# Feed-forward of an attention layer: the second product in row tiles of 128 tokens with a column-tiled remainder

## The chip, the cores and the metric

The program runs on one core of a Trainium2 chip. A core has five engines that run their own instruction streams: TensorE (PE; its weight loads are listed apart as PEld), VectorE (DVE), ScalarE (ACT), GpSimd (POOL) and SyncE (SP), which only issues transfers here. Work passes through an on-chip memory of 128 partitions (SBUF), and TensorE writes its results into a second one (PSUM) of eight banks of 128 partitions by 512 fp32 numbers. Sixteen DMA engines move data between these and the chip's main memory, or within SBUF. Engines wait for one another, and for transfers, on semaphores.

The metric is the time of the whole program on the device in microseconds (us). Before the change three runs gave a median of 3563.27 us, from 3559.06 to 3570.37.

## The reference

Four layers run one after another on x, 16 batches of 100 tokens of 512 channels, all in fp32. Layers 0 and 2 are cross-attentions to a context of 361 tokens a batch, layers 1 and 3 are recurrent layers (a scan over the 100 tokens, with decays, and a channel mixing). The change lies in the last part of layer 2, its feed-forward:

```python
hidden = out + residual
residual = hidden
y = layer_norm(hidden, ln2_w, ln2_b)
y = jax.nn.gelu(y @ fc_w + fc_b, approximate=True)   # 512 -> 2048
y = y @ proj_w + proj_b                              # 2048 -> 512
return residual + y
```

The inputs are a full draw: every weight, bias and scale has values of its own, so nothing of this can be left out.

## The kernel before, in words

The residual x stays in SBUF through all layers as 16 tiles `xb[b]` of 100 partitions (the tokens of a batch) by 512 channels. `layer2_ffn` works on four groups of four batches (`NG = 4`, `G = 4`), so on T = 400 tokens at a time. For each group it does the following.

1. `ln_to_channels` normalizes the four tiles on VectorE (lines 206, 207 and 219) and GpSimd (lines 208 and 209), turns them on TensorE (line 226) so that channels lie on partitions, and evicts the four results to `yT` on ScalarE with scale and bias (line 229).
2. The first product: for each of 16 blocks f of 128 hidden channels, `project` (line 63) adds up four matmuls with 128 columns of `fc` as weights and the 400 tokens as the moving data. ScalarE takes each result through the gelu into `h[:, f, :]` (line 1607). `h` has hidden channels on partitions and the 400 tokens as columns, and one buffer.
3. The second product: for each batch i of the group, `project` adds up 16 matmuls over f. Here the weights are the 100 columns of `h` that belong to the batch, and the moving data are the 512 columns of `proj[:, f, :]`; the result in PSUM has the tokens of the batch on 100 partitions, as `xb` has. GpSimd adds the bias row to x (line 1612), and VectorE adds the result from PSUM to x (line 1617).

Every PSUM result of this stage takes one of eight banks in turn (`mm_tile`). A matmul of fp32 operands in the code is two instructions on TensorE, each with a weight load.

The order of instructions on each engine within this stage is not that of the code: a scheduler places them by their dependences and priorities, so that statistics and normalized rows of later groups are computed on VectorE while the first group is still under way. On TensorE the order is the plain one: transposes, first product, second product of group 0, then of group 1, and so on.

SyncE's queue holds, in this order around the stage: the four loads of `proj` (line 1585) and the small ones, layer 3's Wk, then Wv, Wr, Wg and Wo (line 57), each of which waits for a buffer that a quarter of `fc` holds until the last group's first product has read it, and then what layer 3 begins with: `vec` (line 633), two parts of `maa_w` (lines 655 and 657), `td_w2` and a part of `maa_w2` (lines 660 and 661), `td_w1` (663), `st01` (665) and the state `s0` (667). These take the SBUF space of layer 2's feed-forward, so the first of them waits for the last matmul of the stage.

Layer 3 (`rwkv`) begins with constants on VectorE (lines 680 to 709), the statistics of the first four batches on VectorE and GpSimd (line 77 with the tiles `st_a`, `mv_a`, `ve_a`, `rstd_a`), a rearrangement of `s0` on TensorE (line 82, tile mm) that ScalarE copies to `s0r`, and then, next in ScalarE's queue, the normalized rows `xn_a`.

In the profile's lines a tile is written without its numbers: `p` is the result of the second product, `h` both the first product's bank and the tile it is evicted to, `l_fc` and `l_proj` the weights, `av` the weighted sum of values in layer 2's attention (`attend`), which is computed by groups of 32 columns of weights that go to four different groups of 32 PSUM partitions.

Of the kernel before, what the change touches and what calls it, by code (L numbers as in the profile page):

```python
# [9 lines left out]
F32 = mybir.dt.float32  # L10
U8 = mybir.dt.uint8
AF = mybir.ActivationFunctionType
ALU = mybir.AluOpType
AX = mybir.AxisListType

B, L, E, S2 = 16, 100, 512, 361
NC = E // 128
G = 4
NG = B // G
T = G * L  # L20
# [15 lines left out]
def xattn_sequence(ctx: ExitStack, tc: tile.TileContext, d: dict, out: bass.AP):  # L36
    nc = tc.nc
# [6 lines left out]
    def psum_bank(es, name, bufs):  # L44
        pool = es.enter_context(tc.tile_pool(name=name, bufs=bufs, space=PSUM))
        return lambda n: pool.tile([128, 512], F32, tag="mm", name=n)
# [13 lines left out]
    def project(ps, lhs, rhs, n=NC):  # L60

        for c in range(n):
            nc.tensor.matmul(out=ps, lhsT=lhs(c), rhs=rhs(c), start=(c == 0), stop=(c == n - 1))  # L63
# [148 lines left out]
    def ln_to_channels(pool, g, w, bb, dst, eps, name, bank):  # L212

        rows = [xb[g * G + i] for i in range(G)]
        mv, rstd = ln_stats(pool, rows, eps, name)
        xn = []
        for i in range(G):
            t = pool.tile([L, E], F32, tag="xn", bufs=G + 1, name=f"xn_{name}_{i}")
            nc.vector.tensor_scalar(
                t, rows[i], mv[:, i, 0:1], rstd[:, i : i + 1], ALU.subtract, ALU.mult  # L220
            )
            xn.append(t)
        for c in range(NC):
            ps = bank(f"lnT_{name}_{c}")
            for i in range(G):
                nc.tensor.transpose(
                    ps[:, i * L : (i + 1) * L], xn[i][:, c * 128 : (c + 1) * 128], ident[:L, :L]
                )
            nc.scalar.activation(  # L229
                dst(c), ps[:, :T].rearrange("p (b t) -> p b t", t=L), AF.Identity,  # L230
                bias=bb[:, c : c + 1], scale=w[:, c : c + 1],
            )
# [1056 lines left out]
    def l2_vecs(pool):  # L1289
        t = pool.tile([128, len(L2_VECS), NC], F32, tag="vec2", name="vec2")  # L1290
        nc.sync.dma_start(out=t, in_=d["L2_vec"])
        return {k: t[:, i, :] for i, k in enumerate(L2_VECS)}
# [285 lines left out]
    def layer2_ffn(fc, next_weights):  # L1578
        with ExitStack() as es:
            one = es.enter_context(tc.tile_pool(name="l2b_one", bufs=1))  # L1580
            two = es.enter_context(tc.tile_pool(name="l2b_two", bufs=2))
            mm_tile = psum_bank(es, "l2b_mm", 8)
            proj = one.tile([128, 16, E], F32, name="l2_proj")
            for i in range(4):
                nc.sync.dma_start(
                    out=proj[:, 4 * i : 4 * i + 4, :],
                    in_=d["L2_proj_w"][i * 512 : (i + 1) * 512, :].rearrange("(c p) n -> p c n", p=128),
                )
            vec = l2_vecs(one)
            fcb = one.tile([128, 16], F32, name="fcb")  # L1590
            nc.sync.dma_start(out=fcb, in_=d["L2_fc_b"])
            row = one.tile([L, E], F32, name="l2_pb")
            nc.sync.dma_start(out=row, in_=d["L2_proj_b"].partition_broadcast(L))
            for g in range(NG):
                yT = two.tile([128, NC, T], F32, tag="yT", name=f"yTb_{g}")
                ln_to_channels(
                    two, g, vec["ln2_w"], vec["ln2_b"],
                    lambda c: yT[:, c, :].rearrange("p (b t) -> p b t", t=L), 1e-5, f"l2b_{g}", mm_tile,
                )
                h = two.tile([128, 16, T], F32, tag="h", bufs=1, name=f"h_{g}")  # L1600
                for f in range(16):
                    ps = mm_tile(f"h_{g}_{f}")
                    o = (f % 4) * 128
                    project(
                        ps[:, :T], lambda c: fc[f // 4][:, c, o : o + 128], lambda c: yT[:, c, :]
                    )
                    nc.scalar.activation(
                        h[:, f, :], ps[:, :T], AF.Gelu_apprx_tanh, bias=fcb[:, f : f + 1], scale=1.0
                    )
                for i in range(G):  # L1610
                    x = xb[g * G + i]
                    nc.gpsimd.tensor_tensor(x, x, row, ALU.add)
                    ps = mm_tile(f"p_{g}_{i}")
                    project(
                        ps[:L, :], lambda f: h[:, f, i * L : (i + 1) * L], lambda f: proj[:, f, :], 16
                    )
                    nc.vector.tensor_tensor(x, ps[:L, :], x, ALU.add)  # L1617
            return next_weights()

    def load(layer, *names):  # L1620
# [7 lines left out]
        load_w(d["L2_fc_w"][:, i * 512 : (i + 1) * 512], f"l2_fc{i}") for i in range(4)  # L1628
    ])
    ws3 = layer2_ffn(fc, lambda: load(3, "Wk", "Wv", "Wr", "Wg", "Wo"))  # L1630
    rwkv(3, ws3, lambda: {"": None}, True)

# [64 lines left out]
```

## Time and profile before

| quantity | value |
|---|---|
| runs, median (lowest to highest) | 3563.27 us (3559.06 to 3570.37) |
| the profiled execution's own time | 3563.91 us |
| its span, first to last instruction | 3561.8 us |
| mean granted TensorE clock | 0.937 |
| TensorE busy | 3252.8 us (91% of the span) |
| VectorE, ScalarE, GpSimd busy | 1768.5, 972.8, 1374.2 us |
| second product of layer 2's feed-forward on TensorE | 220.4 us, 512 instructions |
| first product | 175.4 us, 512 instructions |
| stage, first transposes to last matmul | 2294.4 to 2704.1 us |

Busy times overlap among engines and don't add up to the span. A group of instructions is given with its busy time, the mean duration of one instruction, and the time for which its engine was idle before it, with what ended that. Matmuls overlap in TensorE's pipeline: the duration of one (593 ns for 512 columns) is longer than the distance from one start to the next (429 ns). So durations of single matmuls are not added up; the distance of starts is used.

### The profile page before, as it was taken

To read this page: it belongs to the slowest core of one execution; us is meant where nothing else is said; L and a number is where in the kernel's file an instruction comes from. 1 tells how busy PE (TensorE), PEld (TensorE's weight loads), DVE (VectorE), ACT (ScalarE), POOL (GpSimd) and SP (SyncE) were. 2 spreads that over 40 slices of the span, in tenths; PEclk is the share of its full clock that TensorE was granted. 3 is DMA by queue.
4 is the path that set the end of the run, shared out by engine and by line. 5 is a ranking of instruction groups with operands and counts; after the bars stand their busy time and mean duration, and the time that the engine had idled before them with its cause. 6 is when DMAs were issued, how large, how long until landed. Compare 5 with 4: busy or idle time off the path is not lost. (4 is left out here: it accounts for less than half of the span.)

```text
span 3561.8 us, 45408 instructions
## 1 busy us (share of the span) xinstructions
PE 3252.8 (91%) x17411; PEld 1434.5 (40%) x17411; DVE 1768.5 (50%) x3570; ACT 972.8 (27%) x1699; POOL 1374.2 (39%) x1036
## 2 busy tenths in 40 slices
PE   6999998868999988989999999699998899998898
PEld 3444443334333333334455455344443433333333
DVE  4777777723767755523333333400001386775551
ACT  1323222322333333322222322201111233333332
POOL 1444444543666655412212112200002366665541
PEclk8999999978999989989999999899998899998998
DMA  5010101022434342011000010200011243434300
GB/s 167 21 30 21 30 21 33 1 65 82 134 101 136 116 130 77 14 52 35 19 19 19 27 31 21 74 0 0 0 47 49 83 138 101 136 116 119 86 27 16
DMA packets 151074, 213.26 MB, mean 60 GB/s; under 512 B 22942, under 2 KB 131294, under 8 KB 150858
## 3 DMA queue, kind: packets, MB, share of 16 engines
q1 hardware_dynamic: 127818, 177.59, 17.3%
q10 hardware_dynamic: 23040, 32.78, 2.6%
q8 instruction: 137, 2.24, 0.3%
q14 instruction: 79, 0.65, 0.1%
HBM read 174.25 MB, written 36.04 MB: 59 GB/s over the span
## 5 line engine op out<-in xcount | busy, mean ns | idle before, releaser
L77 POOL TENSOR_TENSOR a<-a,rr 128x800 f32<-128x800 f32 x256 | 480.5, 1878 | 342.1 <-DVE a L77 265.4
L77 DVE TENSOR_TENSOR_SCAN a<-wr,vb 128x400 f32<-128x400 f32 x512 | 475.7, 970 | 19.3 <-PE acc L82 9.7
L77 DVE TENSOR_TENSOR vb<-vb,kr 128x792 f32<-128x792 f32 x256 | 250.5, 979 | 197.1 <-ACT vb L77 195.5
L77 DVE CUSTOM_DVE_ANT_0 junk<-l_sc,mask 100x361 f32<-100x361 f32 x512 | 273.0, 533 | 89.9 <-PE l_sc L82 73.4
L82 PE MATMUL vb<-vc,sel 32*128 32x396 f32 x1024 | 260.8, 566 | 2.4 <-ACT th L77 1.3
L77 DVE TENSOR_TENSOR pt<-l_sc,maskT 121x400 f32<-121x400 f32 x384 | 193.5, 566 | 91.9 <-PE l_sc L82 91.0
L77 ACT ACTIVATE pt<-pt 121x1600 f32<-121x1600 f32 x96 | 147.6, 1538 | 284.2 <-DVE pt L77 282.6
L1425 DVE CUSTOM_DVE_ANT_0 junk<-l2a_sc,mask 100x361 f32<-100x361 f32 x256 | 136.9, 535 | 173.0 <-PE l2a_sc L82 155.8
L63 PE MATMUL p<-l_proj,h 128*100 128x512 f32 x512 | 220.4, 593 | 0.0
L77 POOL TENSOR_TENSOR xj<-tm,ext 128x400 f32<-128x400 f32 x160 | 152.5, 960 | 170.3 <-DVE tm L77 165.2
L77 DVE SCALAR_TENSOR_TENSOR tm<-mm,vec,sx 128x400 f32<-128x400 f32 x160 | 99.8, 631 | 229.3 <-PE mm L82 184.3
L1617 DVE TENSOR_TENSOR x<-p,x 100x512 f32<-100x512 f32 x16 | 11.1, 691 | 379.3 <-PE p L63 340.2
L1461 POOL TENSOR_TENSOR pa<-pt,pt 121x1600 f32<-121x1600 f32 x16 | 57.2, 3573 | 366.7 <-ACT pt L1456 366.7
L63 PE MATMUL h<-yTb,l_fc 128*128 128x400 f32 x512 | 175.4, 505 | 7.9 <-ACT yTb L229 7.9
L82 PE MATMUL v<-l_v_w,ct 128*121 128x512 f32 x384 | 179.9, 614 | 0.0
L82 PE MATMUL k<-ct,l_k_w 128*128 128x361 f32 x512 | 172.8, 481 | 7.7 <-DVE mv_l2a L207 7.7
L77 POOL TENSOR_TENSOR pa<-pt,pt 121x1600 f32<-121x1600 f32 x32 | 114.7, 3583 | 167.0 <-ACT pt L77 167.0
L82 PE MATMUL l_sc<-kz,qz 32*100 32x361 f32 x1024 | 116.0, 523 | 42.6 <-DVE pt L77 21.6
L77 ACT COPY vb<-s0r 128x8 f32<-128x8 f32 x256 | 43.1, 168 | 408.7 <-PE vb L82 318.6
L82 PEld LDWEIGHTS vb<-vc,sel 32*128 32x128 f32 x1024 | 85.3, 190 | 145.5 <-issue 105.3
L63 PEld LDWEIGHTS p<-l_proj,h 128*100 128x100 f32 x512 | 85.7, 167 | 133.2 <-issue 132.6
L63 PEld LDWEIGHTS h<-yTb,l_fc 128*128 128x128 f32 x512 | 98.4, 193 | 82.9 <-ACT yTb L229 9.8
(254 smaller groups left out, 5317.3 us busy)
## 6 DMA issues: line engine op xcount, KB each, us to landing
kr<-dk SPq DMA_DIRECT2D x256, 100.0 KB
wr<-dw SPq DMA_DIRECT2D x256, 100.0 KB
rr<-dr SPq DMA_DIRECT2D x256, 100.0 KB
ct<-in_ctxT SPq DMA_DIRECT2D x32, 722.0 KB
dk<-k ACTq DMA_DIRECT2D x32, 200.0 KB
kc<-dk SPq DMA_DIRECT2D x32, 200.0 KB
dw<-wd ACTq DMA_DIRECT2D x32, 200.0 KB
dv<-v ACTq DMA_DIRECT2D x32, 200.0 KB
```

Of the source, the lines that this page charges most:

```text
L63: nc.tensor.matmul(out=ps, lhsT=lhs(c), rhs=rhs(c), start=(c == 0), stop=(c == n - 1))
L77: return lambda *args, **kw: tc.keep_in_program_order(op(*args, **kw))
L82: pin(nc.tensor.matmul(**kw))
L1425: nc.vector.tensor_tensor_reduce(out=junk, in0=ss[r][:L, :S2], in1=t["mask"], scale=-1.0, scalar=FLT_MAX, op0=ALU.add, op1=ALU.min, accum_ ...
L1461: nc.gpsimd.tensor_tensor(t["pa"], t["pt"][0], pt, ALU.add)
L1617: nc.vector.tensor_tensor(x, ps[:L, :], x, ALU.add)
```

## The change

The second product no longer follows the batches. Its 400 tokens a group are cut into three tiles of 128 rows and a remainder of 16.

- Each of the three tiles is added up over f with 128 columns of `h` as weights. ScalarE copies the result from PSUM to a tile `po` in SBUF (three buffers), and transfers on SyncE's queue bring its rows to where their batches have them, in a tile `pb` of 100 partitions by four batches by 512 (one buffer). Each tile has tokens of two batches, so there are two transfers a tile: 100 and 28 rows, 72 and 56, 44 and 84.
- The remainder takes the last 32 columns of `h` as weights (16 of them are computed a second time and not used). Its 512 output columns are cut into four quarters r, and the matmul of quarter r writes PSUM partitions 32r to 32r + 31: four column groups of the array, each with its own copy of the weights and 128 columns of `proj` as moving data. ScalarE copies the 128x128 result to a tile `pr`, and four transfers of 16 rows by 128 columns bring the quarters to `pb`.
- VectorE's adds read `pb` in SBUF in place of the PSUM bank, after GpSimd's add of the bias row as before.

```diff
+                pb = two.tile([L, G, E], F32, tag="pb", bufs=1, name=f"pb_{g}")
+                for i in range(3):
+                    ps = mm_tile(f"p_{g}_{i}")
+                    project(
+                        ps, lambda f: h[:, f, i * 128 : (i + 1) * 128], lambda f: proj[:, f, :], 16
+                    )
+                    t = two.tile([128, E], F32, tag="po", bufs=3, name=f"po_{g}_{i}")
+                    nc.scalar.copy(t, ps)
+                    for b in range(G):
+                        lo, hi = max(b * L, i * 128), min(b * L + L, i * 128 + 128)
+                        if lo < hi:
+                            nc.sync.dma_start(
+                                out=pb[lo - b * L : hi - b * L, b, :], in_=t[lo - i * 128 : hi - i * 128, :]
+                            )
+                ps = mm_tile(f"p_{g}_3")
+                for f in range(16):
+                    for r in range(4):
+                        nc.tensor.matmul(
+                            out=ps[32 * r : 32 * r + 32, :128], lhsT=h[:, f, T - 32 : T],
+                            rhs=proj[:, f, r * 128 : (r + 1) * 128], start=(f == 0), stop=(f == 15),
+                        )
+                t = two.tile([128, 128], F32, tag="pr", name=f"pr_{g}")
+                nc.scalar.copy(t, ps[:, :128])
+                for r in range(4):
+                    nc.sync.dma_start(
+                        out=pb[L - 16 : L, G - 1, r * 128 : (r + 1) * 128], in_=t[32 * r + 16 : 32 * r + 32, :]
+                    )
                 for i in range(G):
                     x = xb[g * G + i]
                     nc.gpsimd.tensor_tensor(x, x, row, ALU.add)
-                    ps = mm_tile(f"p_{g}_{i}")
-                    project(
-                        ps[:L, :], lambda f: h[:, f, i * L : (i + 1) * L], lambda f: proj[:, f, :], 16
-                    )
-                    nc.vector.tensor_tensor(x, ps[:L, :], x, ALU.add)
+                    nc.vector.tensor_tensor(x, pb[:, i, :], x, ALU.add)
```

The order of instructions moves as follows. On TensorE only the matmuls of the second product change. ScalarE has the four copies of a group between the last gelu of that group and the first eviction of the next group's transposes. SyncE has the ten transfers of each of groups 0 to 2 between the loads of layer 3's Wk and Wv; of group 3 the six transfers of whole tiles stand behind Wo, then comes `vec`, then the four transfers of the remainder, then `maa_w` and the others to `s0`. On VectorE the add of batch 15 moves behind layer 3's constants, and stands just ahead of layer 3's first statistics; the adds of batches 3 and 7 move behind normalized rows of later groups. GpSimd's order is the same.

## The prediction

> **What bounds the kernel now.** I read the groups of instructions first, to see on which engine the changed lines lie, then the timeline of the stage, then the place where it hands over to layer 3. First the groups inside the feed-forward (line, engine, operation; busy us and mean ns; then the idle time before them and what ended it):
>
> ```profile
> L63 PE MATMUL p<-l_proj,h 128*100 128x512 f32 x512 | 220.4, 593 | 0.0
> L63 PE MATMUL h<-yTb,l_fc 128*128 128x400 f32 x512 | 175.4, 505 | 7.9 <-ACT yTb L229 7.9
> L1607 ACT ACTIVATE h<-h,fcb 128x400 f32<-128x400 f32 x64 | 38.0, 593 | 132.2 <-PE h L63 132.2
> L1617 DVE TENSOR_TENSOR x<-p,x 100x512 f32<-100x512 f32 x16 | 11.1, 691 | 379.3 <-PE p L63 340.2 <-PE lnT_l2b L226 39.1
> ```
>
> TensorE is never idle before a matmul of the second product; every other engine waits for it. Each fp32 matmul of the program is two instructions (256 in the code, x512 here). The timeline of TensorE over one group of four batches (start us, duration):
>
> ```profile
> 2450.40 55.10 PE L63 MATMUL p<-l_proj,h 128*100 128x512 f32 x128
> 2505.33 1.54 PE L226 MATMUL lnT_l2b<-ident,xn_l2b 100*128 100x100 f32 x16
> 2506.71 43.18 PE L63 MATMUL h<-yTb,l_fc 128*128 128x400 f32 x128
> 2549.72 55.10 PE L63 MATMUL p<-l_proj,h 128*100 128x512 f32 x128
> ```
>
> There is no gap: second product 54.93 us (2505.33 - 2450.40), transposes 1.38, first product 43.01, and again. The stretch from 2451 to 2506 has a granted clock of 1.00. So this stage is bound by TensorE, and what is taken from it there comes off the end, unless the hand-over to layer 3 gives it back:
>
> ```profile
> 2704.27 0.35 SPq L633 DMA_DIRECT2D vec<-in_L_vec  x1
> 2704.66 0.43 SPq L655 DMA_DIRECT2D maa_w<-in_L_maa_w  x1
> ...
> 2707.91 0.38 SPq L667 DMA_DIRECT2D s<-in_s  x1
> 2707.94 0.68 DVE L77 BATCH_NORM_STATS2 st_a<-x 100x6 f32<-100x512 f32 x1
> ...
> 2712.25 1.04 PE L82 MATMUL mm<-s,ident 32*32 32x64 f32 x38 [8.12 <-issue]
> ```
>
> The last matmul ends at 2704.14. SyncE's queue then issues eight loads in a row, s last; TensorE stands 8.1 us until s has landed. This queue is what the change touches second.
>
> **What the skill says.** The Trainium skill, "TensorEngine Tiling (Array Packing)", section Key Properties: tiles of different position load weights and multiply in parallel, but a change of tiling mode drains the array. The same page, Instruction Overhead: a matmul costs some 60 cycles however few columns it has; 128 columns are above that. "TensorE: Matmul & The Clock Gate", Part 3, is more careful: weight loads run ahead of matmuls only where row groups differ, and three column tiles of M=32 gave 2.38 times. The trace has the very pattern of the new tail, four column groups in turn, each with 32 columns of weights, in layer 2's attention, and it decides:
>
> ```profile
> 2222.14 2.28 PE L82 MATMUL av<-pt,v 121*32 121x100 f32 x96
> ```
>
> 96 instructions in 2.28 us are 23.75 ns each. One after another, at the 0.838 ns a column of the second product (429.1 ns / 512), 100 columns are 83.8 ns: the four groups run 3.5 at a time here, weight loads included. Fourteen such blocks at full clock take 2.28 us each.
>
> **The change, part by part, on TensorE.** Per group of four batches:
> - Removed: 64 matmuls with 100 rows, 54.93 us.
> - Added: three tiles of 128 rows, 96 instructions of 512 columns. Time follows the columns streamed and not the width of the weights: the first product has 128-wide weights and needs 43.01 / 128 = 336.0 ns for 400 columns, 0.840 ns each, against 0.838 with 100-wide weights. So 96 x 429.1 ns = 41.2 us.
> - Added: the tail, 64 matmuls, 128 instructions of 128 columns. From below: perfect fourfold overlap, 128 x 107.3 / 4 = 3.4 us. From the nearest row: 23.75 x 1.28 = 30.4 ns each, 3.9 us. From the skill's 2.38 of 3 carried to four groups (3.17 times, an estimate from Part 3): 13.7 / 3.17 = 4.3 us. The av block has shorter streams to hide its loads behind than the tail, so I take 3.8.
> - Two changes of tiling mode a group and the new ScalarE copy ahead of the transposes' evictions: the trace shows 250 ns from start to end of a short matmul (av median 249) as the most a drain costs, and overlaps that are partly kept; 0.15 us a group.
>
> Gain per group 54.93 - 41.2 - 3.8 - 0.15 = 9.8 us; four groups 39.1 us.
>
> **The rest, hidden or not.** ScalarE gets 12 copies of 128x512 (the nearest row, 121x512 copies of line 1409, takes 585 ns) and 4 of 128x128 (under the 374 ns of the 128x256 copies): 8 us in all, where it is busy 0.6 of 55 us; if that cover were gone it would be 2 us a group. In each group the copy of the tail, some 0.3 us from the tail's end, stands before the eviction of the first transposes, which began 0.55 us after the transposes' start (2406.56 against 2406.01): free, or 0.1 us.
>
> SyncE issues ten transfers a group. Those of groups 0 to 2 stand between the loads of layer 3's Wk and Wv; Wv was issued at 2617.0, 10 us after group 3's first product begins, and the last transfer ahead of it then is done some 3 us after group 2 ends. Hidden. Landing: a 200 KB store issued at 2739.61 released its reader at 2741.53, 1.9 us (the skill's "DMA: Bandwidth & Descriptors", Anatomy of one DMA, has about 2.0 fixed, for another issue path). VectorE's adds now wait for these landings. Behind them in its queue stand the normalized rows of later groups: those of group 2 behind the add of batch 2, those of group 3 behind the add of batch 6. They are read one group later, some 45 us; hidden. pb has one buffer; its last reader is done some 50 us before the next group writes it.
>
> The hand-over is not hidden. The transfers of group 3's tail stand behind vec and ahead of maa_w and the rest: 4 issues of 0.35 to 0.5 us, 1.8 us, move s by as much. The add of batch 15 now stands after the constants and just ahead of the statistics: last issue 2.1 us after the end, landing 1.9, add 0.7, so 4.7 us; the statistics began 3.8 us after it (2707.94) and begin 0.9 later. s may also wait for that add, since its load now waits for a transfer and for VectorE, and would go at 5.6 us either way instead of 3.8. So s decides: 2.0 us later (from below 0.9, if only the statistics counted; from above, the second rival). TensorE's and GpSimd's orders in layer 3 are those of before.
>
> Sum: -39.1 + 2.0 = -37.1. The profiled execution took 3563.9 us (span 3561.8, 2.1 around it), 0.6 above the median of 3563.3. 3563.9 - 37.1 = 3526.8; against the median 3526.2. I predict 3526.5.
>
> **Rivals.**
> - *The tail overlaps only in part.* If weight loads into one row group are exposed between rounds, as Part 3 warns, two groups run at once: 6.9 us instead of 3.8, 12 us back, 3539. Against it: the av rate. For it: av's blocks are only 24 rounds long and add up three deep, the tail sixteen.
> - *The hand-over costs more*: the four small transfers (16 rows of 512 B) land late, or a buffer of layer 3 in pb's place waits for the add: s and the statistics 5 to 10 us later, 3530 to 3535.
> - *No gain*: the column groups run one after another, loads hidden. Tail 128 x 107 ns = 13.7 us, what it replaces; +2.6 for the rest, 3566.
> - *Slower*: each instruction of the tail also pays its own weight load. In the av blocks a load is 105 to 110 ns long; 128 x (107 + 108) = 27.5 us a group, 13.8 more than removed; 3563.9 + 55 + 2.6 = 3621. This decides once an instruction of the tail costs over 102 ns, 4.3 times the av rate (13.73 less 0.15 less a quarter of 2.0 us, over 128).
> - *Layer 3 shifts*: its clock falls to 0.50 in stretches of 5 to 10 us (2759 to 2769, for one) after brief idle. Other phases of these move the end by some 5 us either way; the runs of before lie 11 us apart.
>
> **How the numbers follow.** The forecast has 0.70, its own range 3519 to 3533: tail of 3.4 to 4.3 us, hand-over of 1 to 4, and the spread of the runs. Partial overlap 0.11, hand-over 0.13, no gain 0.03, slower 0.03. From 3516 to 3541 holds the first three and their spread, less the far ends. 0.3% (10.7 us) is about what a measurement of this kernel tells from no change: faster 0.94, same 0.03, slower 0.03.
>
> **What would show it.** Three blocks of 96 instructions in all at about 429 ns each, then one of 128 in 3.5 to 4.3 us, then the transposes with no gap; groups 89.5 us apart instead of 99.3. ScalarE's copies with idle time before them ended by TensorE. TensorE standing about 10 us before mm<-s. Wrong would be: a tail above 5 us, transposes waiting for VectorE, a first product waiting for yTb by more than before, Wv issued later than TensorE frees its buffer, or layer 3 longer than its 857 us.

## The result, and the profile after

The changed kernel takes 3527.12 us in the median of four runs (3522.39 to 3530.07) beside 3564.16 us (3559.06 to 3570.37) for the kernel before: a ratio of 0.9894, 95% interval 0.9874 to 0.9914. It is faster by 37 us; 3526.5 was forecast.

The profiled execution is the slowest of those four: 3530.07 us, span 3528.3, 33.5 us less than the span before. These are the groups of instructions in the feed-forward (line, engine, operation, tiles, shape, count; then busy us and mean ns; then idle time before them and what ended it):

```profile
L63 PE MATMUL p<-l_proj,h 128*128 128x512 f32 x384 | 165.4, 592 | 0.0
L1629 PE MATMUL p<-l_proj,h 128*32 128x128 f32 x512 | 14.8, 273 | 0.0
L1619 ACT COPY po<-p 128x512 f32<-128x512 f32 x12 | 7.0, 586 | 157.9 <-PE p L63 157.9
L1642 DVE TENSOR_TENSOR x<-pb,x 100x512 f32<-100x512 f32 x16 | 12.8, 799 | 338.3 <-DMA pb<-po 332.7 <-DMA pb<-pr 5.6
```

The second product has gone from 220.4 us busy to 165.4 + 14.8. As before, TensorE never waits in it. ScalarE waits for TensorE, and VectorE now waits for the transfers. One group on TensorE's timeline (start us, duration):

```profile
2440.25 41.36 PE L63 MATMUL p<-l_proj,h 128*128 128x512 f32 x96
2481.55 3.70 PE L1629 MATMUL p<-l_proj,h 128*32 128x128 f32 x128
2485.18 1.59 PE L226 MATMUL lnT_l2b<-ident,xn_l2b 100*128 100x100 f32 x16
2486.61 43.18 PE L63 MATMUL h<-yTb,l_fc 128*128 128x400 f32 x128
2529.62 41.36 PE L63 MATMUL p<-l_proj,h 128*128 128x512 f32 x96
```

Three tiles take 41.30 us (2481.55 - 2440.25), the tail 3.63, transposes 1.43, the first product 43.01; groups are 89.37 us apart (2529.62 - 2440.25), 9.95 less than the 99.32 before. There is no gap.

The hand-over to layer 3, with E for the end of layer 2's last matmul (2663.98, from where TensorE's wait begins; 2704.13 before). The timeline of SyncE, VectorE and TensorE:

```profile
2664.09 0.36 SPq L633 DMA_DIRECT2D vec<-in_L_vec  x1
2664.56 2.75 SPq L1636 DMA_DIRECT2D pb<-pr  x4
2667.36 0.59 SPq L655 DMA_DIRECT2D maa_w<-in_L_maa_w  x1
...
2668.54 0.69 DVE L1642 TENSOR_TENSOR x<-pb,x 100x512 f32<-100x512 f32 x1 [1.20 <-DMA pb<-pr]
...
2670.81 0.36 SPq L667 DMA_DIRECT2D s<-in_s  x1
...
2674.82 2.86 PE L82 MATMUL mm<-s,ident 32*32 32x64 f32 x128 [10.84 <-POOL shift_a L77]
```

The four issues of the tail's transfers take 2.75 us, and everything behind them in SyncE's queue is that much later or a little more: maa_w at E + 3.38 instead of E + 0.53, s at E + 6.83 instead of E + 3.8. TensorE stands 10.84 us instead of 8.12. (The releaser in brackets is inferred from semaphores. What mm waits for is s: by the trace's semaphores the load of s was complete at E + 10.54, 0.3 us ahead of mm; and before the change mm began ahead of shift_a.)

So the profiled pair divides as follows. From the start to the first product of group 0: 2305.39 and 2305.32 us, no difference. From there to E: 398.74 and 358.66, so -40.1. From E to the end of the span: 857.67 and 864.32, so +6.6. Only 2.7 of these 6.6 us are the longer wait. Behind it the clock differs. In the table of busy times by stretch, one of 5 us each (columns: length, busy time and count of TensorE, its weight loads, VectorE, ScalarE and GpSimd, granted clock, DMA share, GB/s), before has from E + 23:

```profile
2727.20:2732.20 5.00, 4.41 (x13) 1.52 (x13) 0.63 (x1) 0.50 (x1) 0.96 (x1) 1.00 0.00 0
```

and after has from E + 23:

```profile
2687.00:2692.00 5.00, 5.00 (x8) 2.07 (x7) 0.00 (x0) 0.00 (x0) 2.30 (x3) 0.50 0.00 0
```

TensorE is back at full clock there before, and still at half after. This is taken up below.

### The profile page after: what moved, and what is told of

It reads as the page before. It is cut to its first block, busy times and chain, and to the rows that moved or that the text cites. A ratio compares the mean times of both kernels' runs of the same rounds, so it can differ in the third digit from the quotient of the medians.

```text
span 3528.3 us, 46276 instructions
## 1 busy us (share of the span) xinstructions
PE 3217.1 (91%) x17795; PEld 1432.9 (41%) x17795; DVE 1770.8 (50%) x3570; ACT 981.8 (28%) x1715; POOL 1376.4 (39%) x1036
## 5 line engine op out<-in xcount | busy, mean ns | idle before, releaser
L1642 DVE TENSOR_TENSOR x<-pb,x 100x512 f32<-100x512 f32 x16 | 12.8, 799 | 338.3 <-DMA pb<-po 332.7
L63 PE MATMUL p<-l_proj,h 128*128 128x512 f32 x384 | 165.4, 592 | 0.0
L82 PE MATMUL mm<-l_Wo,gc 128*100 128x512 f32 x256 | 124.6, 629 | 8.4 <-POOL gc L77 8.4
L63 PEld LDWEIGHTS h<-yTb,l_fc 128*128 128x128 f32 x512 | 98.1, 192 | 83.3 <-ACT yTb L229 10.1
```

Source lines behind the costliest of these rows:

```text
L82: pin(nc.tensor.matmul(**kw))
L1642: nc.vector.tensor_tensor(x, pb[:, i, :], x, ALU.add)
```

## The experiments

Two theories had to be told apart for the stage (is the tail short because four column groups run at once?), and several for the hand-over (what makes layer 3 begin late?). All times are medians; the kernel before had 3563.5 to 3566.5 us beside them. What an experiment was expected to show is given ahead of it, as theory and rivals. A line of three dots marks what is left out of a diff or a timeline.

### One quarter after the other

```diff
-                for f in range(16):
-                    for r in range(4):
+                for r in range(4):
+                    for f in range(16):
```

> The changed kernel with the two loops of the remainder exchanged: all 16 matmuls of one column group one after another, then the next group. Same matmuls, same transfers. Theory (the remainder is cheap because matmuls that follow each other go to different column groups and run at once): they no longer do, a remainder takes 128 x 107 ns = 13.7 us instead of 3.63, up to 27.5 us if weight loads of 108 ns show too; the whole 3527 + 40 = 3567 us, or up to 3622. Rival (the gain comes from having only three tiles of 512 columns, in whatever order the remainder runs, for instance because its weights are narrow): 3.6 us and 3527 us.

Measured: 3564.57 us (3558.92 to 3568.28), 0.999 of before (0.9981 to 0.9998). The tail on TensorE's timeline:

```profile
2492.23 12.94 PE L1629 MATMUL p<-l_proj,h 128*32 128x128 f32 x128
```

From its start to that of the transposes it takes 12.87 us, 100.5 ns an instruction on average, and the gain is gone. The instructions are the same 128, with the same weights, columns and results; only the order in which they follow one another differs. That four column groups in turn are what makes the tail short is shown by this: 12.87 us become 3.63, 3.5 times faster. The starts of single instructions say how complete the overlap is. In the serial order they are 109 ns apart within a quarter (the mean is lower because some instructions overlap at the three changes from one quarter to the next). In the changed kernel the four of a round start within 20 ns, and rounds are 109 ns apart: each column group goes on at the pace that one group has alone. The weight loads are hidden even in the serial order: each takes 110 ns in the trace, as long as the distance from one instruction to the next, and adds nothing to it.

### The remainder as a plain tile of 16 rows

```diff
...
+                project(
+                    ps[:16, :], lambda f: h[:, f, T - 16 : T], lambda f: proj[:, f, :], 16
+                )
+                t = two.tile([16, E], F32, tag="pr", name=f"pr_{g}")
+                nc.scalar.copy(t, ps[:16, :])
+                nc.sync.dma_start(out=pb[L - 16 : L, G - 1, :], in_=t)
```

> The remainder as a fourth tile of 16 rows with all 512 columns, without column groups, and one transfer of 16 rows. Theory (time follows the columns streamed, not the rows): 32 instructions of 429 ns, 13.7 us, so a group takes 99.3 us as before the change, and the whole 3564 + 2 to 3 us for the hand-over, 3566. Rival (rows count: 16 rows cost less than 100): well below, towards 3527.

Measured: 3564.08 us (3561.81 to 3572.7), 0.9998 of before (0.9989 to 1.0007). The second product of a group on the timeline:

```profile
2450.57 55.20 PE L63 MATMUL p<-l_proj,h 128*128 128x512 f32 x128
```

That is 55.13 us from start to start for 64 matmuls, as with four tiles of 100 rows (54.93). A tile of 16 rows costs as much as one of 100 or 128: TensorE's time here follows the columns that are streamed, and not the rows.

### The way through SBUF alone

The tiles of the kernel before (100 rows, one a batch), but copied to SBUF by ScalarE, brought to `pb` by a transfer on SyncE's queue, and added from there.

```diff
                     ps = mm_tile(f"p_{g}_{i}")
                     project(
                         ps[:L, :], lambda f: h[:, f, i * L : (i + 1) * L], lambda f: proj[:, f, :], 16
                     )
+                    t = two.tile([L, E], F32, tag="po", bufs=3, name=f"po_{g}_{i}")
+                    nc.scalar.copy(t, ps[:L, :])
+                    nc.sync.dma_start(out=pb[:, i, :], in_=t)
...
```

> The kernel before with the new way back alone: batches as tiles, each result copied by ScalarE, brought to pb by one transfer of 100 rows, added from SBUF. Theory: TensorE's stage as before, 99.3 us a group; TensorE stands 9 to 10 us before layer 3's first matmuls instead of 8.1, since one transfer stands ahead of the loads on SyncE; 3564 to 3567 us. Rival (taking VectorE's adds off PSUM, or the earlier release of the banks, is part of the gain): groups shorter than 99.3 us, 3555 or less.

Measured: 3566.86 us (3560.31 to 3570.58), 1.0006 of before (0.9997 to 1.0015). Copies, transfers and later adds cost nothing that shows in the median. The end of the stage on the timeline:

```profile
2705.53 0.50 SPq L665 DMA_DIRECT2D st<-in_st  x1
2706.91 0.69 DVE L1622 TENSOR_TENSOR x<-pb,x 100x512 f32<-100x512 f32 x1 [2.11 <-DMA pb<-po]
2707.63 0.33 SPq L667 DMA_DIRECT2D s<-in_s  x1
```

Here SyncE had issued the load ahead of s, and then stood 1.6 us until the add of batch 15 was done at 2707.60. So s does wait for that add, which the prediction had left open. In the changed kernel SyncE reaches s only at E + 6.83, when the add (done at E + 5.25) is over.

### Two column groups of 64

```diff
-                    for r in range(4):
+                    for r in range(2):
                         nc.tensor.matmul(
-                            out=ps[32 * r : 32 * r + 32, :128], lhsT=h[:, f, T - 32 : T],
-                            rhs=proj[:, f, r * 128 : (r + 1) * 128], start=(f == 0), stop=(f == 15),
+                            out=ps[64 * r : 64 * r + 64, :256], lhsT=h[:, f, T - 64 : T],
+                            rhs=proj[:, f, r * 256 : (r + 1) * 256], start=(f == 0), stop=(f == 15),
...
```

The copy takes 256 columns then, and two transfers of 16 rows replace the four.

> The remainder in two column groups of 64 with 256 columns each instead of four of 32 with 128 (48 of the 64 weight columns are computed a second time and not used). Theory (the groups run at once, so the time is the columns streamed by one group): 64 instructions of 256 columns, 64 x 214.5 / 2 = 6.9 us a remainder, 3.2 more than with four; the whole 3527 + 13 = 3540 us. Rival (one group after another is hidden by something else than overlap, such as shorter streams): 3.6 us or 13.7 us.

Measured: 3538.53 us (3535.85 to 3538.85), 0.9922 of before (0.9907 to 0.9937). The tail:

```profile
2483.98 7.13 PE L1629 MATMUL p<-l_proj,h 128*64 128x256 f32 x64
```

7.06 us from its start to that of the transposes. One, two and four groups give 12.87, 7.06 and 3.63 us: the time goes down nearly with the number of groups.

### The tail's transfers on ScalarE's queue, and the changed kernel beside it

```diff
-                    nc.sync.dma_start(
+                    (nc.scalar if g == NG - 1 else nc.sync).dma_start(
                         out=pb[L - 16 : L, G - 1, r * 128 : (r + 1) * 128], in_=t[32 * r + 16 : 32 * r + 32, :]
```

> The four small transfers of the last group go out on ScalarE's queue instead of SyncE's; the products are those of the changed kernel. E is the end of layer 2's last matmul. Theory A (the prediction's: only the place in SyncE's queue delays s): s is issued at E + 4.0 us, as before the change (3.77), and TensorE stands 8.2 us before mm<-s, 2.6 us less: 3524.5. Theory B (s also waits for the add of batch 15, which is nearly as late): copy at E + 0.5, four issues of 0.6 us to E + 2.9, landing 1.9 us after the last, add 0.7: s at E + 5.3, TensorE stands 9.3 us, 1.5 us less: 3525.6. Theory C (the place in the queue does not matter, what is late is the data): s at E + 6.8 as in the changed kernel, no difference.

The changed kernel itself:

> The changed kernel once more, to be timed beside the three that follow. Theory and rivals say the same here: 3527 us, within 3 us, with 10.8 us of TensorE standing before mm<-s.

Measured: 3527.68 us (3525.94 to 3531.76) beside 3528.90 (3525.56 to 3533.34) for the changed kernel; the runs overlap, and the medians settle nothing. The timeline does:

```profile
2666.41 2.52 ACTq L1636 DMA_DIRECT2D pb<-pr  x4
2671.55 0.69 DVE L1642 TENSOR_TENSOR x<-pb,x 100x512 f32<-100x512 f32 x1 [2.15 <-DMA td_w<-in_L_td_w]
2672.31 0.33 SPq L667 DMA_DIRECT2D s<-in_s  x1
...
2675.76 2.83 PE L82 MATMUL mm<-s,ident 32*32 32x64 f32 x128 [9.70 <-DVE mv_a L77]
```

With E at 2666.06, s is issued at E + 6.25, directly behind the add (2671.55 + 0.69), and TensorE stands 9.70 us: theory B, with the add some 1 us later than it had. (The line names td_w as the releaser of the add; by the semaphores the last small transfer was complete at E + 5.32, and td_w only after the add had begun.) But the add is 0.9 us later than in the changed kernel (E + 5.49 against 4.56), although the transfers were issued at once. From the end of the last issue to the add it took 2.6 us (2671.55 - 2668.93), where it was 1.2 behind SyncE's issue: beside layer 3's loads the small transfers took longer.

### The remainder ahead of the second tile

The last thing to leave the stage is then a whole tile; its two transfers are on ScalarE's queue in the last group. `whole(i)` is one tile of 128 rows with its copy and its transfers.

```diff
...
+                whole(0)
                 ps = mm_tile(f"p_{g}_3")
...
+                whole(1)
+                whole(2)
```

> In each group the 16 left over are computed between the first and the second tile of 128, so that the last thing to leave layer 2 is a whole tile; its two transfers go out on ScalarE's queue in the last group. If the tail's 3.63 us is a matter of the instructions themselves, it stays 3.6 us in the new place, and the group stays at 89.4 us. Theory B (s waits for the add of batch 15): copy of 512 columns to E + 0.9, two issues of 0.75 to 1.0 us to E + 2.6, landing 1.9, add 0.7: s at E + 5.1, TensorE stands about 9.1 us, 1.7 us less than in the changed kernel: 3525.4. Theory A (the queue alone): 8.2 us, 3524.5. Rival: between two full tiles the tail hides its first weight loads less well, 4.3 us a group, +2.7 us in all: 3528.

Measured: 3528.51 us (3524.61 to 3535.46), as the changed kernel. The tail keeps its 3.63 us between two full tiles (2370.84 to 2374.47 in group 0), so the rival of 4.3 falls. TensorE did not stand 9.1 but 10.96 us: the two transfers, 256 KB on ScalarE's queue beside SyncE's loads, released the last add at E + 6.58, and s behind it at E + 7.34. The 1.9 us for a landing, taken from the prediction, didn't hold beside the loads.

### The remainders of all groups pooled

```diff
+                nc.gpsimd.tensor_copy(hk[:, :, 16 * g : 16 * g + 16], h[:, :, T - 16 : T])
...
+                whole(0)
+                if g == NG - 1:
+                    ps = mm_tile("p_rest")
+                    for f in range(16):
+                        for r in range(2):
+                            nc.tensor.matmul(
+                                out=ps[64 * r : 64 * r + 64, :256], lhsT=hk[:, f, :],
+                                rhs=proj[:, f, r * 256 : (r + 1) * 256], start=(f == 0), stop=(f == 15),
+                            )
...
+                whole(1)
+                whole(2)
```

The rows go to a tile `pl` with a slice for the last batch of each group, and the four adds of batches 3, 7, 11 and 15 read it at the end.

> The 16 tokens left over of all four groups are kept (GpSimd copies their rows of h aside) and computed once, in the last group after its first tile, as 64 tokens in two column groups of 64 by 256 columns. Theory (only the columns streamed per instruction and the number of groups count): four tails of 3.63 us, 14.5 us, become one of 7.1 us, as in the run with two column groups of 64; groups 0 to 2 take 85.8 us each, and layer 2 ends 7.4 us earlier. The hand-over is that of a last whole tile on ScalarE's queue, TensorE standing 9 to 9.5 us before mm<-s: in all 9 us less than the changed kernel, 3518. Rival (the hand-over costs more, since the adds of four batches now stand together at the end): TensorE stands 13 us or more, 3522.

Measured: 3522.43 us (3516.60 to 3526.45), 0.9877 of before (0.986 to 0.9894). From the first product to E it takes 351.31 us, 7.35 less than the changed kernel, as expected. TensorE stands 11.41 us at the hand-over instead of 9 to 9.5: again two large transfers on ScalarE's queue beside the loads, the last add at E + 7.27 and s at E + 8.10. With those two transfers left on SyncE's queue:

> As the run with the pooled remainders, but the last tile's two transfers stay on SyncE's queue, ahead of the loads of layer 3 instead of beside them on ScalarE's queue. Theory (what made the hand-over of that run 11.4 us was that the two transfers shared the DMA engines with layer 3's loads, so that they landed over 3 us after their issue, and s waited for the add behind them): the two issues cost SyncE 1.6 us, they land 1.9 us after their issue, the add of batch 15 ends at about E + 5.2, s is issued at E + 5.5 to 6, and TensorE stands 9.5 to 10 us: 1.5 to 2 us less than with ScalarE's queue. Rival (the landing is slow in itself, since a transfer of 84 rows takes over 3 us wherever it is issued): s at E + 8 as before, TensorE stands 11.4 us or more, no difference.

and the changed kernel beside it:

> The changed kernel beside the run above, on the same chip, for a closer comparison. Theory: the pooled remainders save three tails and 1 us of hand-over, 8 us; so this one is 8 us slower than the run above, 3527 against 3519, and TensorE stands 10.8 to 11.5 us before mm<-s. Rival (what the pooling takes from the tails is lost again at the hand-over or to the clock of layer 3): the two within 3 us.

Measured: 3514.12 us (3510.50 to 3516.36), 0.9858 of before (0.9843 to 0.9872), against 3530.52 (3522.57 to 3534.56), 0.9909 (0.9892 to 0.9925). All runs of the one are below all runs of the other. The hand-over:

```profile
2652.15 0.43 SPq L655 DMA_DIRECT2D maa_w<-in_L_maa_w  x1
2652.68 0.79 SPq L1629 DMA_DIRECT2D pb<-po  x1
2653.51 0.81 SPq L1629 DMA_DIRECT2D pl<-po  x1
...
2656.68 0.68 DVE L1659 TENSOR_TENSOR x<-pl,x 100x512 f32<-100x512 f32 x1
2657.44 0.33 SPq L667 DMA_DIRECT2D s<-in_s  x1
...
2661.46 2.85 PE L82 MATMUL mm<-s,ident 32*32 32x64 f32 x128 [9.77 <-DMA s<-in_s]
```

E is at 2651.69; the add ends at E + 5.67, s goes at E + 5.75, TensorE stands 9.77 us, as the theory had it: here SyncE's queue costs less than ScalarE's. The medians lie 16 us apart where 8 were expected; the two profiled spans lie 8.6 apart, 7.3 of it in the stage and 3.0 behind E, less 1.7 that arose ahead of the stage, in code that is the same. The profiled run of the changed kernel was the fastest of its four, so the traces don't show the rest of the 16 us. The mean granted clock of the runs points to it: 0.938 in that run, 0.935 in its three others, 0.938 to 0.939 in the four of the pooled kernel. By an estimate 0.003 of 3528 us is some 21 us more at half clock, worth about 7 us by the traces below.

### s on ScalarE's queue, and the small transfers issued twice

The three traces of the changed kernel all have some 864 us from E to the end, where before had 857.7. Two last runs were meant to make the wait shorter and longer.

```diff
-            nc.sync.dma_start(out=s0, in_=d["s0"])
+            (nc.scalar if n == 3 else nc.sync).dma_start(out=s0, in_=d["s0"])
```

> The changed kernel, with the load of s in layer 3 issued on ScalarE's queue; everything else stays where it is. s then waits only for the add of batch 15 (done at E + 5.25, E being the end of layer 2's last matmul) and is issued at about E + 5.3 instead of 6.83; TensorE stands 9.3 to 9.7 us before mm<-s instead of 10.8 to 11.6. Theory (a longer wait at the hand-over also lengthens the stretch at half clock behind it, and so costs about twice its length): from E to the end 860 us, as in the runs that stood 9.6 to 10.1 us, 4 us less than the changed kernel's 864: 3525 to 3526. Rival (the wait costs what it lasts, and the rest of layer 3's 864 us comes from elsewhere, from the transfers left in the batches' rows, say): from E to the end 862.4, 1.5 us less.

```diff
-                for r in range(4):
+                for r in [0, 1, 2, 3] * (2 if g == NG - 1 else 1):
                     nc.sync.dma_start(
```

> The changed kernel, with the four small transfers of the last group issued twice (the same rows, the same data), so that SyncE's queue reaches s some 2.8 us later, and the add of batch 15 comes later too. s is issued at E + 9.6 to 10.5, and TensorE stands 13.6 to 14.5 us. Theory (a longer wait also lengthens the stretch at half clock): from E to the end 864 + 2.8 and as much as 3 more, 867 to 870. Rival (it costs what it lasts): 867. If the stretch at half clock ends at a fixed time after the first matmul of layer 3, this run and the one beside it should differ from the changed kernel by the wait alone.

Measured: 3529.13 us (3526.01 to 3533.55) and 3526.30 (3520.70 to 3530.09), not to be told apart from the changed kernel. The first, with E at 2665.65:

```profile
2669.03 0.59 SPq L655 DMA_DIRECT2D maa_w<-in_L_maa_w  x1
2671.06 0.36 ACTq L667 DMA_DIRECT2D s<-in_s  x1
2676.89 2.85 PE L82 MATMUL mm<-s,ident 32*32 32x64 f32 x128 [11.24 <-DMA td_w<-in_L_td_w]
```

s was issued at E + 5.41, 1.4 us earlier than in the changed kernel, and TensorE stood 11.24 us all the same: what both sides had expected of the wait was wrong. By its semaphore the load of s was complete at E + 10.89, 5.5 us behind its issue, where it took 3.7 in the changed kernel. From the issue of maa_w to mm it took 7.86 us. In before it was 7.59, in the three traces of the changed kernel 7.46, 8.10 and 8.23. The loads from maa_w to s have 1472 KB together, and they share the DMA engines; the Trainium skill says so ("DMA: Bandwidth & Descriptors", Issuing engines are not separate DMA queues: transfers run on the same 16 engines whoever issues them, and other queues save only the issuing). This trace agrees: in each of the four us from 2671.03 on, the profile puts the mean busy share of the 16 engines at 0.91 to 1.06. So what the tail's transfers delay in the changed kernel is the start of the whole block of loads, and an earlier place for s among them gains nothing. A later place does cost: with the tail's transfers on ScalarE's queue the block began at E + 0.53, as before the change, but s went only at E + 6.25, behind the add, and TensorE still stood 9.70 us. Both limits lie close together here.

In the second the four extra transfers came between maa_w and the loads behind it. TensorE stood 14.12 us, as expected, and from E to the end it took 866.84 us, 2.5 to 3.3 more than the changed kernel: what the wait lasts, and no more. That is the rival.

### What comes on top of the wait

All traces side by side; stage is from the first product of group 0 to E, half clock the stretch at clock 0.50 that begins 2 to 5 us behind E, found in the granted clock of stretches of 0.2 us; all in us:

| kernel | stage | wait for mm | half clock | E to the end |
|---|---|---|---|---|
| before | 398.74 | 8.12 | 20.6 | 857.67 |
| way through SBUF alone | 399.14 | 9.59 | 20.6 | 857.02 |
| 16 rows | 399.56 | 9.62 | 20.4 | 859.98 |
| tail's transfers on ScalarE's queue | 358.74 | 9.70 | 20.6 | 860.04 |
| pooled, SyncE's queue | 351.51 | 9.77 | 20.6 | 860.51 |
| two column groups | 372.36 | 10.08 | 20.4 | 859.91 |
| changed | 358.66 | 10.84 | 23.8 | 864.32 |
| remainder early | 359.65 | 10.96 | 23.8 | 862.77 |
| s on ScalarE's queue | 358.78 | 11.24 | 24.0 | 863.55 |
| pooled, ScalarE's queue | 351.31 | 11.41 | 24.0 | 863.74 |
| one quarter after the other | 395.69 | 11.45 | 27.4 | 864.12 |
| changed, second and third trace | 358.55, 358.80 | 11.48, 11.60 | 24.0, 23.8 | 864.16, 863.53 |
| small transfers twice | 358.66 | 14.12 | 27.2 | 866.84 |

The half clock lasts 6, 7 or 8 times 3.41 us, and nothing between. The Trainium skill has this ("TensorE: Matmul & The Clock Gate", Part 1: the clock is full or half, and is set by how busy TensorE was in windows of some 3.4 us that run freely); 20.5, 23.9 and 27.3 us agree with it. Up to a wait of 10.1 us it is six windows; from 10.8 on it is seven or eight. A window more at half clock can cost as much as 1.7 us of TensorE's work (half of 3.41). The eight traces with waits of over 10.8 us have on average 2.2 us more behind their first matmul than the four with waits of 9.6 to 10.1 and some 860 us (852.5 against 850.3, E to the end less the wait); three of them (the first of the changed kernel, the serial quarters, the small transfers twice) have a further 3.4 us at half clock some 7 us later.

The clock records of the whole stretch from E to the end show more. The four traces with the shorter wait have 158.7 to 158.9 us at half clock in it, the eight with the longer one 162.3 to 169.2, on average 7.5 more. Over all 14 traces the time behind the first matmul follows this sum, by 0.31 us for each us at half clock (correlation 0.95), which makes 2.3 us of 7.5. So the windows are enough to account for the 2.2 us. This is a correlation with mostly one trace a kernel. What lengthens the later half-clock stretches, and whether a longer wait always does, is not shown: the longest wait, 14.12 us, has no more behind its first matmul than the first trace of the changed kernel (852.72 against 853.46). The clock also moves code that is the same everywhere: the first product of group 0 began between 2298.47 and 2311.28 us, and the later the more time at half clock lay ahead of it (264 to 298 us, correlation 0.90).

## Why the prediction was right, and where it was not

**The bound and the tiles: right.** TensorE set the stage, and what was taken from it there came off. Three tiles: 41.2 us forecast, 41.30 measured. Time by columns and not by rows is shown by the tile of 16 rows.

**The tail: right, a little too dear.** 3.8 us forecast (3.4 to 4.3), 3.63 measured. The av block was misread: 96 instructions in 2.28 us counts in the 0.25 us that the last one takes by itself. Its starts are 21.4 ns apart, so it runs 3.9 at a time and not 3.5, and 21.4 x 1.28 is 27.4 ns a tail instruction; 27.0 were measured, and some 0.2 us pass from the last start to the transposes. Perfect overlap, the lower bound of 3.4 us, was nearly reached. Of the three bounds, the one from the Trainium skill ("TensorE: Matmul & The Clock Gate", Part 3: 2.38 times with three column tiles, from which 3.17 for four was estimated) was the furthest off, at 4.3; here the whole tail is 3.5 times shorter than in the serial order. The condition that Part 3 states there, that loads run ahead only where row groups differ, is not borne out: all four groups use the same rows of the array, and no load shows. The attention's av block, which the forecast went by, was the better measure even as it was read.

**Mode changes and the copy of pr: 0.15 us a group forecast.** The transposes take 1.43 us instead of 1.38, so 0.05; what the changes cost beside this lies within the 41.30 and the 3.63. The gain is 9.95 a group, 40.1 in the stage, where 39.1 was forecast.

**The hand-over: mechanism half right, size wrong.** "s decides: 2.0 us later" is the step that failed. First the issue was mis-sized: the four transfers of 16 rows within SBUF kept SyncE 2.75 us, 0.69 each on average (0.55 to 0.58 of issuing, and a pause of 0.4 behind the first), where 1.8 in all was taken and put at 2.0, from 0.35 to 0.5 for a load out of main memory. Those are durations; the prediction's own lines have eight loads from 2704.27 to 2707.91, 0.52 us from one start to the next, which would have made 2.1. Then it isn't s alone that is late but the whole block of loads from maa_w on (moved from E + 0.53 to E + 3.38), and s would have come no sooner from an earlier place in it, as the run with s on the other queue shows. And behind the wait, which grew by 2.7 to 3.5 us in three traces, the half clock lasts a window longer, which the sum had put at nothing. From E to the end this makes 5.9 to 6.6 us, where 2.0 was forecast and 1 to 4 allowed, and the prediction's own sign for being wrong, layer 3 longer than its 857 us, was there. That s may wait for the add of batch 15 was right, and shown by the way through SBUF alone; in the changed kernel the add is over before the queue reaches s.

**The sum.** The three traces of the changed kernel give, on average, -40.1 + 6.3 = -33.8; the forecast was -37.1. That the four runs of the first comparison gave -37.0 was luck: a hand-over 4.3 us too dear was offset by 1.0 us in the stage, and for the rest by runs that happened to be fast. The twelve runs of the changed kernel in the three comparisons have a median of 3529.7 us, 3 us above the forecast and well inside its range. The size is that of the rival *the hand-over costs more*, but in the changed kernel neither of the two causes named there: the last small transfer released its add 1.8 us after its issue began, and no load of layer 3 was held up by the add, though s was in six of the runs above (the plain tile of 16 rows, the way through SBUF alone, the tail's transfers on ScalarE's queue, the remainder early, and both pooled kernels).

**The other rivals.** Partial overlap (6.9 us a tail), no gain (13.7) and slower (27.5) are excluded by 3.63. What two groups at once and one after the other would have cost is now measured, 7.06 and 12.87; the fourth, a load paid by every instruction, did not come about even in the serial order. The last, *layer 3 shifts*, had its part: behind their first matmul the three traces of the changed kernel have 2.4 to 3.9 us more than before, with 6.8 to 7.8 us more at half clock.

**The rest held.** Groups 0 to 2: Wv was issued at 2586.94, 11 us after group 3's first product began, as before (it was 11 there too, and not the 10 of the prediction). First product and transposes waited for nothing new.

## What to carry to other kernels

A remainder of few rows cost TensorE as much here as a full tile (16 rows and 128), because its time follows the columns streamed. Cut over four column groups, with the groups interleaved instruction by instruction, it cost about a quarter, 3.63 us instead of 13.7; pooled over four rounds it was paid once. Count what such a change adds to the queue of the next stage at the price of the very kind of transfer, from start to start: four small issues ahead of a block of loads delayed the whole block by 2.85 us, and to issue one of the loads earlier on another queue gained nothing while the DMA engines were busy. When a wait of TensorE grows, look at the granted clock behind it too: it changed in whole windows, and the time behind the wait went with it.

## What the hardware showed that was not expected

- Transfers within SBUF hold SyncE for longer than loads: 0.55 to 0.59 us for 16 rows of 512 B, 0.75 to 1.16 us for 28 to 100 rows of 2 KB, against 0.33 to 0.6 us for layer 3's loads in the same queue. These are durations of single issues in the changed kernel.
- Transfers on ScalarE's queue that ran beside SyncE's loads came later than the same transfers in SyncE's queue with only vec and maa_w ahead of them. In the pooled kernel, from the first issue to the add that waited for it: 5.2 us on ScalarE's queue (2660.25 to 2665.43), 3.4 on SyncE's (2652.68 to 2656.07).
- The stretch at half clock had lengths of 20.4 to 20.6, 23.8 to 24.0 and 27.2 to 27.4 us, in steps of 3.4.
- Four column groups on the same rows of the array ran with no loss: a round of four instructions of 128 columns every 109 ns, as one instruction every 109 ns in one column group. That is 0.85 ns a column, beside 0.838 in instructions of 512 columns. Where the serial order goes from one column group to the next, instructions overlap too, so its mean is 100.5 ns.
